# Loads of the later projections issued one or two pairs ahead, and attention of batch 1 entered before batch 0's ends

## The chip, the cores and the metric

The kernel runs on one core of a Trainium2 chip. The metric is the device time of one execution in microseconds (us), as the median of several runs; lower is better. Profiles come from one execution that the hardware profiler recorded.

## The reference

The input x has the shape (batch 4, time 512, 128, 64) in float32. Each (128, 64) slice is a row of D = 8192 features, so x is also (4, 512, 8192). Layer 0 is a sequence model:

```python
xn = layernorm(x.reshape(b, t, d), ln_attn_g, ln_attn_b)
k = xn @ Wk; v = xn @ Wv; r = sigmoid(xn @ Wr)       # 8192 -> 64
s = decay * s + k_t * v_t                            # scan over time -> states
x = x + r * states @ Wo                              # 64 -> 8192
x = x + gelu(conv(layernorm(x), freq_W) + freq_b)    # 3 taps along the 128, 64 -> 64 channels
x = x + layernorm(causal_conv(layernorm(x), time_W) + time_b)   # 3 taps along time, depthwise
x = x + gelu(x @ ffn_W1 + ffn_b1) @ ffn_W2 + ffn_b2  # 64 -> 256 -> 64
```

Layer 1 takes a 25-wide moving average over time off x, transforms the rest with a DFT to 128 modes, multiplies them by complex matrices (one for each of 64 channels), transforms back and adds the average. The change doesn't touch it.

## The kernel before

Layer 0 works on one batch at a time in feature-major tiles: 128 features on the partitions, 512 time steps along them, 64 such chunks in a batch, taken two at a time, so that a batch has 32 pairs. Its stages are Python generators that yield from time to time with a weight for the TensorE work just written:

- J, `project` (L321): the k, v and r projections. Each pair loads its weights (`wkvr`, L342 or L346; from batch 2 on one load for two pairs, 512 KB, into the tag wx with two buffers), the feature-major input (`load_x`, L293, tag xp with three buffers), and a token-major tile of the same input (L349) from which `bn_stats` (L353, two of them, one for each block of 128 tokens) takes the layer norm's statistics. Four scalings of the weights by the norm's gain (L369) and eight matmuls into one PSUM accumulator (L372, each pair's written as four) follow. In batches 2 and 3 the token-major tile lies in the buffers x2 (even pairs) and sq (odd pairs) of the pool `bk`, two buffers each, so that pair k uses the buffer of pair k-4.
- Z, `scan` (L383): `bn_aggr` (L391) makes mean and variance of the statistics, POOL the inverse root (`rsqrt`, L231 and L232), `rows` spreads them over the partitions with TensorE (`spread`, L240) and copies them out with ScalarE (L284), VectorE corrects k, v and r and runs the scan; the moments of the next norm follow from small matmuls (L467, L468).
- A, `attend_and_convolve` (L478): first `rows` for the norm's scale and shift, then for each pair i `attend(i)` (L494 on TensorE, the residual sum L496 and z L500 on VectorE), `convolve(i-2)` (L515, L524, L529; GELU on ScalarE L530, residual L532, squares L535) and `add_up` of pair i-3 (L250), which sums values and squares over the features on TensorE into the accumulator `st`. There is one accumulator bank ("s") for it. When the last sum is out, `begin` is set to b + 1 (L555) and `finish` (L258 to L267) and `moments` give the next norm: the sums are copied out, L262 picks them, L267 copies them as `me`, then come var, `rs` on POOL and mrs.
- C, `convolve_time`, O, `open_feed`, and F, `feed_forward` (L669): the causal convolution with its norm, and the feed-forward part: L678 widens, L682 is the GELU, L689 narrows into the one PSUM buffer "p", L694 evicts it as `x4t` (VectorE), L703 transposes it, and ScalarE copies it out (L710, L712). `convolve_ahead` (L589) does the first fourteen pairs of the next batch's causal convolution inside F; its norm is spread with L240 into "p" too.

`in_turn` (L748) interleaves two lanes of such stages over the list at L788: attention of batch b + 1 runs beside the causal convolution of batch b, projection and scan of batch b + 2 beside the feed-forward part of batch b. A lane steps when its share of work done is behind the other's. Attention of batch 1 may begin only once `begin` is 1, so after the last `add_up` of batch 0.

TensorE executes in the order in which the program is written (`manual_schedule`). On the other engines a scheduler chooses the order, except for instructions given to `keep_in_program_order`: in batches 2 and 3 that is the first `bn_stats` of each pair, not the second. Loads go out on SP's queue in the order that the scheduler gives them, stores on POOL's. An engine executes its instructions in order, so that all that stands behind a waiting one waits too. A load waits for its buffer's last reader.

Of the kernel before, what the change touches and what calls it, by code (L numbers as in the profile page):

```python
# [10 lines left out]
F32 = mybir.dt.float32  # L11
# [5 lines left out]
P = 128  # L17
# [5 lines left out]
SL = 512  # L23
NS = D // SL
NPR = NCH // 2
NT = T // P
S = 64
# [52 lines left out]
def layer0(ctx, tc, dram, x, xt, vecs, wkvr, wo, wdec, wconv, fbias, w1, fb1, w2, fb2, x4):  # L80
# [4 lines left out]
    nc = tc.nc  # L85
# [17 lines left out]
    def two(pool, tag):  # L103
        return pool.tile([P, 2, SL], F32, tag=tag, name=tag)
# [210 lines left out]
    begin = {}  # L315
# [5 lines left out]
    def project(b):  # L321
        pa = two(ps_m, "m") if b == 1 else two(ps_a, "a")
        held[0] = b == 1
        if b == 0:
            psum_w = ps_p.tile([P, SL], F32, tag="p", name="psum_w")
        stt = rowp.tile([P, NT, NS, 6], F32, tag="stt", name="stt")
        for i in range(NPR):
            first, last = i == 0, i == NPR - 1
            if unscanned[0]:

                wq, xk = two(fr, "x1")[:, :, 0 : 4 * S + 3], spare("z", SL)
            elif b == 1:

                both = spare("wx", 4 * S + SL)
                wq, xk = both[:, :, 0 : 4 * S], both[:, :, 4 * S :]
            else:

                xk = two(bk, "sq" if i % 2 else "x2")
                if i % 2 == 0:
                    pairs = spare("wx", 4 * S + SL).rearrange("p k n -> p (k n)")[:, 0 : 16 * S]  # L340
                    pairs = pairs.rearrange("p (c s) -> p c s", c=4)
                    nc.sync.dma_start(pairs, wkvr[2 * i : 2 * i + 4, :, 0 : 4 * S].rearrange("c p s -> p c s"))  # L342
                wq = pairs[:, i % 2 * 2 : i % 2 * 2 + 2, :]
            if b < 2:
                n = 4 * S + 2 * (b == 0)
                nc.sync.dma_start(wq[:, :, 0 : n], wkvr[2 * i : 2 * i + 2, :, 0 : n].rearrange("c p s -> p c s"))  # L346
            xp = load_x(b, i)
            s, h = i // 2, i % 2 * 2
            nc.sync.dma_start(  # L349
                xk, x[b, h * P : (h + 2) * P, s * SL : (s + 1) * SL].rearrange("(t p) d -> p t d", p=P)  # L350
            )
            for t in range(2):
                stats = nc.vector.bn_stats(stt[:, h + t, s, :], xk[:, t, :])  # L353
                if b > 1 and t == 0:

                    tc.keep_in_program_order(stats)
            if b == 0:
                nc.gpsimd.memset(wq[:, :, n:], 1.0)
                for j in range(2):
                    c = 2 * i + j  # L360

                    w = wq[:, j, :]
                    nc.tensor.matmul(
                        psum_w[0 : S + 2, 0 : 4 * S + 3], lhsT=w[:, 3 * S : 4 * S + 2], rhs=w,
                        start=c == 0, stop=c == NCH - 1,
                    )
            for j in range(2):
                w = wq[:, j, 0 : 3 * S]
                nc.vector.tensor_scalar_mul(w, w, vec[:, G1, 2 * i + j : 2 * i + j + 1])  # L369
            for j in range(2):  # L370
                for k in range(2):
                    nc.tensor.matmul(  # L372
                        pa[:, k, :], lhsT=wq[:, j, k * P : (k + 1) * P], rhs=xp[:, j, :],
                        start=first and j == 0, stop=last and j == 1,
                    )
                yield 1.0
        kvrg = rowp.tile([P, 2, SL], F32, tag="kvrg", name="kvrg")
        nc.scalar.copy(kvrg, pa)
        held[0] = False
        projected[b] = (kvrg, stt, psum_w) if b == 0 else (kvrg, stt)  # L380
# [96 lines left out]

    def attend_and_convolve(b):  # L478
        rst, rs, mrs = scanned.pop(b)
        rb, mb = yield from rows(of_a, rs, mrs, "rm")  # L480

        nc.vector.tensor_scalar(mb, mb, at_one[:, 1:2], at_one[:, 0:1], ALU.mult, ALU.add)
        st = ps_s.tile([P, SL], F32, tag="s", name="st")
        free_s[0] = False
        x1s, zs, ws, waiting = {}, {}, {}, {}

        def attend(i):
            xp = load_x(b, i)
            wo_sb = fr.tile([P, P], F32, tag="wo", name="wo_sb")
            nc.sync.dma_start(wo_sb, wo[:, i, :])  # L490
            at = two(ps_a, "a")
            for j in range(2):
                js = slice(j * S, (j + 1) * S)
                nc.tensor.matmul(at[:, j, :], lhsT=wo_sb[js, :], rhs=rst[js, :], start=True, stop=True)  # L494
            x1 = x1s[i] = fr.tile([P, 2, SL], F32, tag="x1", name="x1")
            nc.vector.tensor_tensor(x1, at, xp, ALU.add)  # L496
            z = fr.tile([P, 2, SL], F32, tag="z", name="z", bufs=4)
            for j in range(2):
                zs[2 * i + j] = z[:, j, :]
            nc.vector.tensor_tensor(z, x1, pair_of(rb), ALU.mult)  # L500

        def scaled(i):

            wcs = fr.tile([P, 2, P + H], F32, tag="wcs", name="wcs")
            for j in range(2):
                c = 2 * i + j
                ws[c] = wcs[:, j, :]
                nc.scalar.mul(wcs[:, j, :], wc_sb[:, i % 2, :], vec[:, G2, c : c + 1])

        def convolve(i):  # L510
            cv = c_bank() if i % 2 or held[0] else two(ps_m, "m")
            for h in range(2):
                for j in range(2):
                    q = 32 * (2 * h + j)
                    nc.tensor.matmul(  # L515
                        cv[h * H : (h + 1) * H, j, :], lhsT=cgr[q : q + 2, i, :], rhs=mb[q : q + 2, :],
                        start=True, stop=False,
                    )
            for j in range(2):
                c = 2 * i + j  # L520
                for n, h in neighbours(i % 2, c):
                    if 0 <= n < NCH:
                        rs = halves[rows_of(n // 2 % 2, n - c)]
                        nc.tensor.matmul(  # L524
                            cv[halves[h], j, :], lhsT=ws[n][rs, P:], rhs=zs[n][rs, :], start=False, stop=False
                        )
            for j in range(2):
                c = 2 * i + j
                nc.tensor.matmul(cv[:, j, :], lhsT=ws[c][:, 0:P], rhs=zs[c], start=False, stop=True)  # L529
            nc.scalar.activation(cv, cv, AF.Gelu_apprx_tanh)  # L530
            x2 = two(bk, "x2")
            nc.vector.tensor_tensor(x2, cv, x1s.pop(i), ALU.add)  # L532
            nc.gpsimd.dma_start(x2d[b][2 * i : 2 * i + 2].rearrange("c p t -> p c t"), x2)
            sq2 = bk.tile([P, 2, SL], F32, tag="sq", name="sq2")
            nc.scalar.activation(sq2, x2, AF.Square)  # L535
            for c in (2 * i - 2, 2 * i - 1):
                zs.pop(c, None)
                ws.pop(c, None)
            if i + 2 < NPR:
                scaled(i + 2)  # L540
            waiting[i] = x2, sq2

        for i in range(2):
            scaled(i)
        for i in range(NPR + 3):
            if i < NPR:
                attend(i)
                yield 1.0
            if 1 < i < NPR + 2:
                convolve(i - 2)  # L550
                yield 5.0
            if i > 2:
                add_up(st, i - 3, *waiting.pop(i - 3), i == 3, i == NPR + 2)
                yield 1.0
        begin[attend_and_convolve], free_s[0] = b + 1, True  # L555
        mean3, sq3 = yield from finish(st, of_a, 3)
        carried[b] = moments(mean3, sq3, 3)
# [181 lines left out]


    CHAIN = 6.0

    def run(b, stages):
        for stage, share in stages:
            for weight in stage(b):
                yield weight * share / whole[stage]

    def in_turn(leads, *pairs):  # L748
        at, running = [0.0, 0.0], [None, None]

        def step(k):
            n = int(at[k])
            b, *stages = pairs[n][k]
            if running[k] is None:
                first = stages[0][0]
                if first in needed and b not in needed[first] or begin.get(first, b) < b:
                    return False
                running[k] = run(b, stages)
            share = next(running[k], None)
            if share is None:  # L760
                running[k] = None
                at[k] = n + 1.0
            else:
                at[k] = min(at[k] + share, n + 0.999)
            return True
# [331 lines left out]
```

## Time and profile before

| what | value |
|---|---|
| median of 3 runs | 3829.72 us (3828.04 to 3830.18) |
| the profiled execution: its time | 3831.03 us |
| its span, first to last instruction | 3829.3 us |
| mean granted TensorE clock | 0.981 |
| waits of TensorE on x4t at L689, whole run | 55.3 us in 55 |
| waits of VectorE at `bn_stats` (L353) for the sq loads | 88.2 us in 26 |
| waits of VectorE at `bn_stats` (L353) for the x loads | 56.1 us in 24 |
| waits of VectorE at the scaling (L369) for wx | 81.2 us in 35 |

Engines in the profile: PE is TensorE (PEld its weight loads), DVE VectorE, ACT ScalarE, POOL GpSimd, SP SyncE, whose queue (SPq) issues loads. A number such as L353 is a line of the kernel before. A group such as `stt<-sq` names output and input by the program's names; the token-major tiles of a projection in batches 2 and 3 appear as x and sq. The table of waits lists for an engine, a line and a releaser the total in us, the count and the longest. In a timeline, a line has the start in us from the span's start, the length, the engine and the instruction, and in brackets the idle time ahead of it with what ended it. Busy time is an average over stages with different limits, so stretches of the span are looked at apart. In this execution batch 0's attention ends near 510 us, batch 2's projection runs from about 811 to 1190 us beside batch 0's feed-forward part, and batch 3's begins near 1540 us beside that of batch 1.

### The profile page before, as it was taken

How to read it: one execution, taken by the hardware profiler on the slowest of the kernel's cores; microseconds unless marked ns; L12 is line 12 of the kernel's file. 1: busy time of each engine (PE TensorE's matmuls, PEld its weight loads, DVE VectorE, ACT ScalarE, POOL GpSimd, SP SyncE). 2: the span in 40 equal slices, each digit the busy share in tenths (PEclk: the TensorE clock that was granted, in tenths of full speed). 3: DMA queues.
4: the chain of work that ended last, by engine and by line, in shares of the span. 5: the costliest groups of instructions: out<-in, count | busy, mean ns of one | idle time of the engine just before them, and what ended most of it. 6: DMA issues, size and time to landing. Idle time of an engine off the chain costs nothing. (4 is left out here: it accounts for less than half of the span.)

```text
span 3829.3 us, 44885 instructions
## 1 busy us (share of the span) xinstructions
PE 3620.5 (95%) x15945; PEld 1342.4 (35%) x15945; DVE 2683.1 (70%) x3498; ACT 1763.0 (46%) x2491; POOL 512.9 (13%) x782
## 2 busy tenths in 40 slices
PE   9999998989999999999989988999989999999999
PEld 4433322233333223333322322333322743327533
DVE  4445669975667896677789699845558268892677
ACT  0023346645556565556746578867744210142100
POOL 0000012210001221011121121100013001121001
PEclk9999999999999999999989999999999999999999
DMA  9867647786775687777568677645558368994687
GB/s 311 276 205 242 223 173 250 260 282 229 246 257 182 233 280 271 251 268 278 188 236 290 209 252 256 210 161 179 182 197 285 130 219 292 312 308 148 199 298 263
DMA packets 429175, 912.80 MB, mean 238 GB/s; under 512 B 33240, under 2 KB 83608, under 8 KB 424856
## 3 DMA queue, kind: packets, MB, share of 16 engines
q1 hardware_dynamic: 350656, 636.65, 49.4%
q0 software_dynamic: 75776, 271.62, 20.4%
q8 instruction: 127, 2.08, 0.2%
q10 hardware_dynamic: 2520, 1.67, 0.1%
q14 instruction: 96, 0.79, 0.1%
HBM read 641.31 MB, written 268.50 MB: 238 GB/s over the span
## 5 line engine op out<-in xcount | busy, mean ns | idle before, releaser
L689 PE MATMUL pa<-mid,w_sb 128*64 128x512 f32 x2048 | 499.7, 609 | 55.5 <-DVE x4t L694 55.3
L682 ACT ACTIVATE mid<-m,fb_sb 128x1024 f32<-128x1024 f32 x256 | 285.1, 1114 | 265.2 <-PE m L678 265.0
L694 DVE SCALAR_TENSOR_TENSOR x4t<-pa,fb_sb,x 128x512 f32<-128x512 f32 x252 | 187.7, 745 | 225.6 <-PE pa L689 225.6
L678 PE MATMUL m<-x,w_sb 64*128 64x512 f32 x1008 | 289.4, 647 | 0.8 <-ACT mid L682 0.4
L682 ACT ACTIVATE mid<-c,fb_sb 128x1024 f32<-128x1024 f32 x256 | 283.2, 1106 | 1.0 <-PE c L678 0.9
L678 PE MATMUL c<-x,w_sb 64*128 64x512 f32 x1008 | 263.7, 596 | 9.8 <-ACT mid L682 9.8
L689 PEld LDWEIGHTS pa<-mid,w_sb 128*64 128x64 f32 x2048 | 124.9, 136 | 398.9 <-issue 216.5
L372 PE MATMUL a<-xp,wx 128*128 128x512 f32 x512 | 244.9, 605 | 0.5 <-DVE me L267 0.5
L965 PE MATMUL b<-xin,avg_sb 128*128 128x512 f32 x512 | 230.8, 593 | 3.3 <-DVE xin L971 3.3
L942 ACT COPY two<-a 128x512 f32<-128x512 f32 x64 | 37.5, 586 | 424.7 <-PE a L937 424.7
L971 DVE TENSOR_TENSOR xin<-b,pm 128x512 f32<-128x512 f32 x256 | 159.1, 684 | 95.7 <-PE b L968 80.8
L535 ACT ACTIVATE sq<-x 128x1024 f32<-128x1024 f32 x128 | 135.0, 1055 | 185.6 <-DVE x L532 184.2
L580 DVE SCALAR_TENSOR_TENSOR to<-kd,vec,to 128x510 f32<-128x510 f32 (+1 forms) x272 | 198.2, 748 | 15.1 <-ACT to L576 11.0
L655 ACT ACTIVATE kd<-kd,vec 128x512 f32<-128x512 f32 x256 | 193.3, 809 | 3.1 <-DVE kd L647 3.1
L847 DVE COPY xf<-b 128x256 f32<-128x256 f32 x128 | 54.4, 425 | 189.1 <-PE b L911 188.5
L250 PE MATMUL st<-x,ones 128*32 128x512 f32 x512 | 171.0, 613 | 14.7 <-DVE x L532 14.7
L703 PEld LDWEIGHTS pt<-ident,x4t 128*128 128x128 f32 x1024 | 108.0, 141 | 208.7 <-ACT mid L682 142.8
L494 PE MATMUL a<-rst,wo_sb 64*128 64x512 f32 x512 | 151.8, 667 | 29.5 <-DVE x L496 26.8
L580 DVE SCALAR_TENSOR_TENSOR z<-x,vec,z 128x511 f32<-128x511 f32 x240 | 175.9, 746 | 5.3 <-ACT z L576 2.3
L868 DVE TENSOR_TENSOR uv<-xin 128x1024 f32<-128x1024 f32 x128 | 155.3, 1228 | 33.9 <-DMA edge<-x 13.9
L496 DVE TENSOR_TENSOR x<-a,xp 128x1024 f32<-128x1024 f32 x128 | 156.4, 1222 | 29.3 <-PE a L494 26.5
L703 PE MATMUL pt<-ident,x4t 128*128 128x128 f32 x1024 | 169.0, 288 | 1.5 <-ACT ob L710 1.5
(241 smaller groups left out, 6506.6 us busy)
## 6 DMA issues: line engine op xcount, KB each, us to landing
xp<-in_xt SPq DMA_DIRECT2D x256, 512.0 KB
xin<-x SPq DMA_DIRECT2D x128, 1024.0 KB
kh<-to SPq DMA_DIRECT2D x156, 512.0 KB
x<-x POOLq DMA_DIRECT2D x128, 512.0 KB, 4.5
kx<-x SPq DMA_DIRECT2D x128, 512.0 KB
x<-ob POOLq DMA_DIRECT2D x64, 1024.0 KB, 6.1
out<-xin POOLq DMA_DIRECT2D x64, 1024.0 KB, 6.9
x<-x SPq DMA_DIRECT2D x96, 512.0 KB
```

Of the source, the lines that this page charges most:

```text
L250: nc.tensor.matmul(st[32 * q : 32 * q + 32, :], lhsT=ones, rhs=src[:, j, :], start=first, stop=last,)
L372: nc.tensor.matmul(pa[:, k, :], lhsT=wq[:, j, k * P : (k + 1) * P], rhs=xp[:, j, :], start=first and j == 0, stop=last and j == 1,)
L496: nc.vector.tensor_tensor(x1, at, xp, ALU.add)
L580: tap = nc.vector.scalar_tensor_tensor(to[:, j, k:], xr[:, j, : SL - k], vec[:, w, c], to[:, j, k:], ALU.mult, ALU.add)
L655: tc.keep_in_program_order(nc.scalar.activation(d[:, j, :], d[:, j, :], AF.Identity, bias=vec[:, B4, c], scale=vec[:, G4, c]))
L678: nc.tensor.matmul(pm[:, h, :], lhsT=w1_sb[hs, m * P : (m + 1) * P], rhs=x3[hs, :], start=True, stop=True)
L682: nc.scalar.activation(mid, pm, AF.Gelu_apprx_tanh, bias=fb1_sb[:, m : m + 1])
L689: nc.tensor.matmul(pa[h * H : (h + 1) * H, :], lhsT=w2_sb[:, m, :], rhs=mid[:, h, :], start=(m == 0), stop=(m == 1),)
L694: nc.vector.scalar_tensor_tensor(x4t, pa, fb2_sb, x3s[c // 2][:, c % 2, :], ALU.add, ALU.add)
L703: nc.tensor.transpose(pt[:, t, :], x4t[:, t * P : (t + 1) * P], ident)
L965: nc.tensor.matmul(po[j], lhsT=avg_sb[:, j, :], rhs=xin[:, j, :], start=True, stop=False)
L971: nc.vector.tensor_tensor(by_n(xin[:, j, :]), by_n(po[j]), by_c(pm[j % 2][:, j // 2, :]), ALU.add)
```

## The change

It has two parts.

In `project`, batches 2 and 3 issue their loads in another order. The token-major load of pair i still goes out in step i, but its two `bn_stats` are written two pairs later, in step i + 2 (the last steps' together at the end). The weights of pairs i + 2 and i + 3 are loaded in step i, and `load_x` of pair i + 1 in step i, so that both are ahead of their use by two pairs and one. Buffers and their numbers are as before, and so is the mark that keeps the first `bn_stats` of a pair in program order. Batches 0 and 1 are as they were.

In `attend_and_convolve`, batch 1 may begin before batch 0's attention is done. `begin` gets values between b and b + 1: 0.25 when batch 0's step 32 is done and 0.75 after step 33, 1 at the end. A stage that may not go on yet yields BLOCKED, and `in_turn` then steps the other lane. Batch 1's `rows` are no longer held back by `begin`, its steps 0, 1, 2 and 3 need `begin` at 0.25, 0.5, 0.75 and 1. Its `rows` use another tag, `rm4`, since batch 0 still reads `rm`; and the accumulator `st` is allocated at step 3, when the bank is free again.

```diff
--- before.py
+++ after.py
@@ -324,36 +324,60 @@
         if b == 0:
             psum_w = ps_p.tile([P, SL], F32, tag="p", name="psum_w")
         stt = rowp.tile([P, NT, NS, 6], F32, tag="stt", name="stt")
-        for i in range(NPR):
-            first, last = i == 0, i == NPR - 1
-            if unscanned[0]:
-
-                wq, xk = two(fr, "x1")[:, :, 0 : 4 * S + 3], spare("z", SL)
-            elif b == 1:
-
-                both = spare("wx", 4 * S + SL)
-                wq, xk = both[:, :, 0 : 4 * S], both[:, :, 4 * S :]
-            else:
-
-                xk = two(bk, "sq" if i % 2 else "x2")
-                if i % 2 == 0:
-                    pairs = spare("wx", 4 * S + SL).rearrange("p k n -> p (k n)")[:, 0 : 16 * S]
-                    pairs = pairs.rearrange("p (c s) -> p c s", c=4)
-                    nc.sync.dma_start(pairs, wkvr[2 * i : 2 * i + 4, :, 0 : 4 * S].rearrange("c p s -> p c s"))
-                wq = pairs[:, i % 2 * 2 : i % 2 * 2 + 2, :]
-            if b < 2:
-                n = 4 * S + 2 * (b == 0)
-                nc.sync.dma_start(wq[:, :, 0 : n], wkvr[2 * i : 2 * i + 2, :, 0 : n].rearrange("c p s -> p c s"))
-            xp = load_x(b, i)
+        def token_major(i, xk):
             s, h = i // 2, i % 2 * 2
             nc.sync.dma_start(
                 xk, x[b, h * P : (h + 2) * P, s * SL : (s + 1) * SL].rearrange("(t p) d -> p t d", p=P)
             )
+            return xk
+        def statistics(i, xk):
+            s, h = i // 2, i % 2 * 2
             for t in range(2):
                 stats = nc.vector.bn_stats(stt[:, h + t, s, :], xk[:, t, :])
                 if b > 1 and t == 0:
 
                     tc.keep_in_program_order(stats)
+        def weights(i):
+            if i < NPR:
+                w = spare("wx", 4 * S + SL).rearrange("p k n -> p (k n)")[:, 0 : 16 * S]
+                w = w.rearrange("p (c s) -> p c s", c=4)
+                nc.sync.dma_start(w, wkvr[2 * i : 2 * i + 4, :, 0 : 4 * S].rearrange("c p s -> p c s"))
+                for k in range(2):
+                    ws[i + k] = w[:, 2 * k : 2 * k + 2, :]
+        ws, xps, xks = {}, {}, {}
+        if b > 1:
+            weights(0)
+            xps[0] = load_x(b, 0)
+        for i in range(NPR):
+            first, last = i == 0, i == NPR - 1
+            if b > 1:
+                xks[i] = token_major(i, two(bk, "sq" if i % 2 else "x2"))
+                if i % 2 == 0:
+                    weights(i + 2)
+                if not last:
+                    xps[i + 1] = load_x(b, i + 1)
+                wq, xp = ws.pop(i), xps.pop(i)
+                for k in (i - 2, NPR - 2, NPR - 1) if last else (i - 2,):
+                    if k in xks:
+                        statistics(k, xks.pop(k))
+            else:
+                if unscanned[0]:
+                    wq, xk = two(fr, "x1")[:, :, 0 : 4 * S + 3], spare("z", SL)
+                else:
+                    both = spare("wx", 4 * S + SL)
+                    wq, xk = both[:, :, 0 : 4 * S], both[:, :, 4 * S :]
+                n = 4 * S + 2 * (b == 0)
+                nc.sync.dma_start(wq[:, :, 0 : n], wkvr[2 * i : 2 * i + 2, :, 0 : n].rearrange("c p s -> p c s"))
+                xp = load_x(b, i)
+                statistics(i, token_major(i, xk))
...
@@ -477,11 +501,9 @@
 
     def attend_and_convolve(b):
         rst, rs, mrs = scanned.pop(b)
-        rb, mb = yield from rows(of_a, rs, mrs, "rm")
+        rb, mb = yield from rows(of_a, rs, mrs, "rm4" if b == 1 else "rm")
 
         nc.vector.tensor_scalar(mb, mb, at_one[:, 1:2], at_one[:, 0:1], ALU.mult, ALU.add)
-        st = ps_s.tile([P, SL], F32, tag="s", name="st")
-        free_s[0] = False
         x1s, zs, ws, waiting = {}, {}, {}, {}
 
         def attend(i):
@@ -540,18 +562,26 @@
                 scaled(i + 2)
             waiting[i] = x2, sq2
 
-        for i in range(2):
-            scaled(i)
         for i in range(NPR + 3):
+            while begin[attend_and_convolve] < b + (min(i, 3) - 3) / 4:
+                yield BLOCKED
+            if i < 2:
+                scaled(i)
             if i < NPR:
                 attend(i)
                 yield 1.0
             if 1 < i < NPR + 2:
                 convolve(i - 2)
                 yield 5.0
+            if i == 3:
+                st = ps_s.tile([P, SL], F32, tag="s", name="st")
+                free_s[0] = False
             if i > 2:
                 add_up(st, i - 3, *waiting.pop(i - 3), i == 3, i == NPR + 2)
                 yield 1.0
+            if b == 0 and i >= NPR and i < NPR + 2:
+                begin[attend_and_convolve] = b + (0.25 if i == NPR else 0.75)
         begin[attend_and_convolve], free_s[0] = b + 1, True
         mean3, sq3 = yield from finish(st, of_a, 3)
         carried[b] = moments(mean3, sq3, 3)
@@ -739,11 +769,12 @@
 
 
     CHAIN = 6.0
+    BLOCKED = -1.0
 
     def run(b, stages):
         for stage, share in stages:
             for weight in stage(b):
-                yield weight * share / whole[stage]
+                yield BLOCKED if weight == BLOCKED else weight * share / whole[stage]
 
     def in_turn(leads, *pairs):
         at, running = [0.0, 0.0], [None, None]
@@ -753,10 +784,12 @@
             b, *stages = pairs[n][k]
             if running[k] is None:
                 first = stages[0][0]
-                if first in needed and b not in needed[first] or begin.get(first, b) < b:
+                if first in needed and b not in needed[first]:
                     return False
                 running[k] = run(b, stages)
             share = next(running[k], None)
+            if share == BLOCKED:
+                return False
             if share is None:
                 running[k] = None
                 at[k] = n + 1.0
```

## Prediction

> **What bounds the kernel now.** I read, in this order, the page's busy table, the clock, the table of waits of the whole run, and then the stages one by one, because a share over the whole span hides which stage has idle time to give back.
>
> ```profile
> PE 3620.5 (95%) x15945; PEld 1342.4 (35%) x15945; DVE 2683.1 (70%) x3498; ACT 1763.0 (46%) x2491; POOL 512.9 (13%) x782
> ```
>
> TensorE is busy for 3620.5 of 3829.3 us; only 209 us can be won by removing waits. A second reserve is the clock, granted at 0.981 on average: about 73 us (0.019 of the span). In the table of stretches the columns are: stretch, its length, busy time of PE, PE's loads, DVE, ACT, POOL, granted clock, DMA share, GB/s.
>
> ```profile
> 507.30:519.30 12.00, 7.04 (x37) 2.82 (x32) 5.02 (x5) 4.00 (x7) 0.73 (x1) 1.00 0.22 72
> 519.30:529.50 10.20, 9.75 (x24) 2.49 (x26) 4.07 (x4) 0.10 (x1) 0.00 (x0) 0.50 0.40 142
> ...
> 817.80:826.40 8.60, 3.62 (x12) 2.55 (x12) 3.09 (x11) 0.59 (x1) 1.26 (x2) 0.61 0.74 251
> 900.00:1150.00 250.00, 229.26 (x891) 82.46 (x890) 166.53 (x222) 135.99 (x183) 23.69 (x28) 1.00 0.74 252
> ...
> 1650.00:1900.00 250.00, 249.79 (x1009) 93.06 (x1008) 183.16 (x243) 158.41 (x213) 28.52 (x34) 1.00 0.73 256
> ```
>
> Four places concern this change: the passage from attention of batch 0 to that of batch 1 (507 to 530), the start of batch 2's projection (818 to 826), the body of that stage (900 to 1150, PE idle for 20.7 us), and batch 3's projection (1650 to 1900), where PE is idle for 0.2 us, so nothing that the change does inside it can gain. The waits in 900 to 1150 name the cause of the third (engine, line, releaser; total, times, longest):
>
> ```profile
> DVE stt L353 <- DMA sq<-in_x: 54.8, 9, 7.4
> ...
> DVE stt L353 <- DMA x<-in_x: 26.3, 9, 3.6
> ...
> PE pa L689 <- DVE x4t L694: 15.1, 17, 2.0
> ```
>
> VectorE stands at `bn_stats` for the token-major load, x4t (L694) is queued behind it, and TensorE waits for x4t, since L689 has a single PSUM buffer. The timeline shows one such stall; times are start, length, and the wait before it in brackets:
>
> ```profile
> 1001.75 0.68 DVE L353 BATCH_NORM_STATS2 stt<-sq 128x6 f32<-128x512 f32 x1
> 1009.87 0.69 DVE L353 BATCH_NORM_STATS2 stt<-sq 128x6 f32<-128x512 f32 x1 [7.43 <-DMA sq<-in_x]
> 1010.48 0.73 DVE L694 SCALAR_TENSOR_TENSOR x4t<-pa,fb_sb,x 128x512 f32<-128x512 f32 x1
> ```
>
> The load into sq is issued at 1002.47, as the `bn_stats` that frees its buffer ends, and VectorE's next instruction already needs that load.
>
> **What the Trainium skill says.** "TensorE: Matmul & The Clock Gate", Part 1: The HAM clock gate, says that an array left idle drops to half rate, decided in windows of about 3.4 us. The trace agrees on the window: its half-clock stretches last 3.4, 6.8 or 10.2 us. The page's section on HAM oscillation asks for gaps under about 3.4 us; here the trace is stricter, as two gaps of 1.33 us at 517 and 520 preceded 10.2 us at half clock. "DMA: Bandwidth & Descriptors", Anatomy of one DMA, gives about 2.0 us plus bytes over 436 GB/s (fitted on the software path): an estimate of 3.2 us for 512 KB. The x loads agree (waits up to 3.6 us); sq, queued behind others, takes up to 7.4.
>
> **Part by part.** The sum is made against the profiled execution, 3831.03 us (span 3829.3 and 1.7 around it), which lies 1.3 us above the median. Instruction counts on every engine are unchanged, so only waits and clock are priced. I read the changed order from the built program.
>
> *A. Batch 1's attention inside batch 0's last pairs.* TensorE passed from one batch to the next like this:
>
> ```profile
> 509.09 1.04 PE L250 MATMUL st<-x,ones 128*32 128x512 f32 x2 [1.36 <-DVE x L532]
> ...
> 511.17 1.16 PE L240 MATMUL a<-ident,rs 128*128 128x128 f32 x8
> 513.00 1.16 PE L240 MATMUL a<-ident,mrs 128*128 128x128 f32 x8 [0.68 <-ACT rm L284]
> 514.84 1.13 PE L494 MATMUL a<-rst,wo_sb 64*128 64x512 f32 x4 [0.68 <-ACT rm L284]
> 517.29 1.13 PE L494 MATMUL a<-rst,wo_sb 64*128 64x512 f32 x4 [1.33 <-DVE x L496]
> 519.75 2.08 PE L494 MATMUL a<-rst,wo_sb 64*128 64x512 f32 x4 [1.33 <-DVE x L496]
> 521.76 1.98 PE L515 MATMUL m<-rm,cgr 2*64 2x512 f32 x8
> ```
>
> Idle: 1.36 + 0.68 + 0.68 + 1.33 + 1.33 = 5.38 us. In the new order both spreads (L240) stand before attends of batch 0's last pairs. The first must wait for POOL's rs: I put it at 1.2 us, as TensorE reaches it at about 485.8 and rs is due near 487. Each copy of rm still costs the next attend 0.68, since the bank is the same. Batch 1's first attend now fills the gap ahead of the last sums, of whose 1.36 about 0.45 is left; its second attend waits no longer, its third still does. 1.2 + 0.68 + 0.68 + 0.45 + 1.33 = 4.34: gain 1.0. The gaps are now spread over 30 us with dense work between, so I expect 3.4 us at half clock in place of 10.2: half of 6.8 is 3.4. Part A: -4.4, with bounds 0 (the clock drops as before) and -6.4 (none left at half clock: 1.0 + 5.1, and 0.3 for the estimate of rs). Nothing on other queues moves but two ACT copies.
>
> *B. Start of batch 2's projection.* The opened program issues five statistics loads where it issued seven ahead of the second weights, so these are the eighth load in the queue, not the ninth. This matters because of what stands behind them on DVE:
>
> ```profile
> 820.33 0.32 DVE L369 TENSOR_SCALAR wx<-wx,vec 128x192 f32<-128x192 f32 x1 [2.28 <-DMA wx<-in_wkvr]
> 820.57 0.16 DVE L267 COPY me<-p 128x8 f32<-128x8 f32 x1
> ...
> 822.82 2.08 PE L240 MATMUL p<-ident,rs 128*128 128x128 f32 x8 [4.98 <-POOL rs L232]
> ```
>
> `me` is behind the scaling of wx; me, var, rs and the spread follow. Nine loads from 801.2 to 820.3 are 2.1 us each; one less brings `me` forward by at most that: I take 1.8, as TensorE's L262 ends soon before. The half clock that follows (6.8 us) stays. Later, a stall of 3.1 us at 846 has no counterpart and one of 2.2 at 866 shrinks, of which I credit TensorE 1.0. Part B: -2.8, bounds 0 (another load takes the place) and -7.0 (the whole 4.98, and 2).
>
> *C. The body of batch 2's projection.* Statistics two pairs behind should give each load 25 us. But in the new order, as in the old, the second, unpinned `bn_stats` of pair k-4 stands directly ahead of the first, pinned one of pair k. The load of pair k needs the buffer which that one frees, so VectorE again meets the load just issued. On SP the steady order is the same but for one xp that goes ahead of a kx. The 20.7 us therefore stay: 0. Two more stalls (one sq, one x) come at the end, where the old order had its loads done. In the body a pair of them costs TensorE 20.7 over some ten periods of 25 us, about 2.1; I take +2.4, bounds 0 and +3. The statistics that end two pairs later are read by `bn_aggr` with 9 us to spare (rs at 1190.8, its spread at 1199.69): hidden. In batch 3 the same stalls are under a busy TensorE (0.2 us in 250): 0; without that cover they would cost the same 2.4.
>
> *D. Start of batch 3's projection.* The timelines of VectorE and TensorE have VectorE late here:
>
> ```profile
> 1557.92 0.69 DVE L353 BATCH_NORM_STATS2 stt<-sq 128x6 f32<-128x512 f32 x1 [4.04 <-DMA sq<-in_x]
> 1558.54 0.73 DVE L694 SCALAR_TENSOR_TENSOR x4t<-pa,fb_sb,x 128x512 f32<-128x512 f32 x1
> ...
> 1559.32 1.16 PE L240 MATMUL p<-ident,rs 128*128 128x128 f32 x8 [2.81 <-DVE x4t L694]
> ```
>
> With the first statistics two pairs later, VectorE is spared its waits of 2.00, 0.44 and 4.04 here. TensorE's gaps of 0.68 and 2.81 go (-3.5), and the 3.4 us at half clock that follow at 1560 (-1.7). Part D: -5.2, bounds 0 (the stalls come back one period later and collide with the same spread) and -10 (also the later gaps, 2.37 and 0.92, and the half clock at 1625).
>
> Sum: -4.4 - 2.8 + 2.4 - 5.2 = -10.0, so 3831.0 becomes 3821.0; from the median, 3819.7. The bounds sum to -23.4 and +3.0: 3806.3 to 3832.7.
>
> **Rivals.** (1) Only the places move: the clock drops as before in A, the stalls of B and D recur one period later, C's two are paid. Then -1.0 + 2.4 and nothing else: 3829.7 + 1.4 = 3831. For it: VectorE's total wait does not shrink. Against: the gaps in D rest on a burst of loads which is gone. (2) The change does in C what its words say: the loads land early, 20.7 us in 250 scales to about 25 over the stage, and with the sum above the time is about 3792. For it: order on VectorE is chosen by the scheduler and stalls of x are short. Against: the order puts freeing and using instruction side by side. (3) Slower: xp is now issued right behind sq and wx, and shares the queues with sq. A period on VectorE is 16.7 us of work and 81.1 / 9 = 9.0 of stall, 25.7 us against TensorE's 25; so VectorE is the bound already and each further us of sq's wait is paid. If one 512 KB transfer, 2.1 us, is added in each of 11 periods: +23, less 10 from elsewhere, 3843; it decides as soon as sq's mean wait exceeds 6.1 us (54.8 / 9) by about 1.6 us, where it eats the forecast's gain and reaches +0.2%. Against: xp comes behind sq in the queue, and the DMA share is 0.74.
>
> **Chances.** Forecast 0.56, rival 1 0.28, rival 2 0.04, rival 3 0.12. A measurement can tell about 0.2%, 7.7 us, from no change: faster is below 3822.1, slower above 3837.4. Of the forecast 0.02 falls within. Faster 0.54 + 0.04 = 0.58; same 0.28 + 0.02 = 0.30; slower 0.12. The range 3806 to 3833 is that of the bounds; it holds the forecast and rival 1 and leaves out 0.16.
>
> **What would show it.** Right: in batch 2's stage VectorE still waits about 80 us in 250 at `bn_stats`, sq over x two to one; gaps of about 4 us around A and at most 3.4 us at half clock there; the wait of 4.98 near 3; no wait of 2.81 at batch 3's start. Wrong: `bn_stats` waits that vanish (rival 2), sq waits with a mean of 8 (rival 3), or half-clock time over the whole run that is not shorter by 8 us or more.

## The result: no change, and the profile after

| | before | after |
|---|---|---|
| median of 12 runs | 3828.54 us | 3828.30 us |
| lowest to highest | 3818.39 to 3840.51 | 3819.37 to 3833.78 |
| profiled execution's span | 3829.3 us | 3826.0 us |
| granted clock | 0.981 | 0.981 |

The ratio is 0.9998, with a 95% interval of 0.9988 to 1.0008; a second comparison (below) gave 1.0002, 0.9990 to 1.0014. The forecast was 3819.7, a gain of 10; its range of 3806 to 3833 holds the result, and its first rival ("only the places move", 3831) is nearest to what came. "Same" had been given a chance of 0.30, "faster" 0.58.

In the changed kernel's numbering L494 is L516, L353 is L337, L369 is L393, L689 is L719 and L694 is L724. The busy table first:

```profile
PE 3622.6 (95%) x15945; PEld 1339.1 (35%) x15945; DVE 2681.4 (70%) x3498; ACT 1762.5 (46%) x2491; POOL 510.4 (13%) x782
```

The work is the same. Now the stretches of after that answer to those of before (stretch, length, busy PE, PEld, DVE, ACT, POOL, clock, DMA share, GB/s): the passage between the batches, the start of batch 2's projection, its body, and batch 3's.

```profile
483.40:515.20 31.80, 29.05 (x165) 9.90 (x164) 12.28 (x16) 14.00 (x22) 4.34 (x6) 1.00 0.31 106
515.20:526.00 10.80, 9.43 (x42) 2.42 (x46) 7.29 (x7) 2.57 (x3) 0.72 (x1) 1.00 0.67 208
809.50:818.00 8.50, 5.87 (x26) 4.00 (x26) 5.04 (x12) 0.58 (x1) 1.26 (x2) 0.80 0.62 201
900.00:1150.00 250.00, 228.57 (x888) 82.00 (x887) 167.36 (x224) 136.60 (x183) 23.98 (x28) 1.00 0.74 249
...
1650.00:1900.00 250.00, 249.52 (x1006) 92.56 (x1004) 188.29 (x249) 158.54 (x213) 28.52 (x34) 1.00 0.73 253
```

The body of batch 2's stage has TensorE idle for 21.4 us of 250, as before (20.7). The waits in it, by releaser:

```profile
DVE stt L337 <- DMA sq<-in_x: 53.3, 9, 6.8
...
DVE stt L337 <- DMA x<-in_x: 30.7, 10, 3.1
...
PE pa L719 <- DVE x4t L724: 15.1, 17, 1.6
```

54.8 and 26.3 have become 53.3 and 30.7, and TensorE's 15.1 is 15.1. The timeline of VectorE shows the same pair of instructions as before (start, length; the wait before in brackets), and SP's queue the load between them:

```profile
1015.42 0.68 DVE L337 BATCH_NORM_STATS2 stt<-sq 128x6 f32<-128x512 f32 x1
1022.06 0.69 DVE L337 BATCH_NORM_STATS2 stt<-sq 128x6 f32<-128x512 f32 x1 [5.96 <-DMA sq<-in_x]
1022.67 0.73 DVE L724 SCALAR_TENSOR_TENSOR x4t<-pa,fb_sb,x 128x512 f32<-128x512 f32 x1
```

```profile
1016.13 0.37 SPq L329 DMA_DIRECT2D sq<-in_x  x1
```

The load still goes out as the freeing `bn_stats` ends (1016.1), and the next instruction of VectorE still needs it. That the statistics are written two pairs later has only moved both. The two halves of a tile are read far apart: counted through the loads into sq of this stage, the tile freed at 1016.1 went out at 961.6 and had its first `bn_stats` at 967.0, and its second, which the scheduler may place, stands 48 us behind the first.

The passage between the batches, on TensorE:

```profile
488.15 1.16 PE L240 MATMUL a<-ident,rs 128*128 128x128 f32 x8 [1.10 <-POOL rs L232]
489.98 1.13 PE L516 MATMUL a<-rst,wo_sb 64*128 64x512 f32 x4 [0.68 <-ACT rm L284]
...
497.82 1.13 PE L516 MATMUL a<-rst,wo_sb 64*128 64x512 f32 x4 [0.68 <-ACT rm L284]
...
515.14 1.05 PE L250 MATMUL st<-x,ones 128*32 128x512 f32 x2 [0.30 <-DVE x L554]
...
519.67 1.13 PE L516 MATMUL a<-rst,wo_sb 64*128 64x512 f32 x4 [1.33 <-DVE x L518]
```

1.10 + 0.68 + 0.68 + 0.30 + 1.33 = 4.09 us of idle where there were 5.38. The start of batch 2's projection and that of batch 3's:

```profile
809.89 0.55 DVE L393 TENSOR_SCALAR wx<-wx,vec 128x192 f32<-128x192 f32 x2 [3.59 <-DMA wx<-in_wkvr]
810.35 0.16 DVE L267 COPY me<-p 128x8 f32<-128x8 f32 x1
```

```profile
812.60 1.16 PE L240 MATMUL p<-ident,rs 128*128 128x128 f32 x8 [2.63 <-POOL rs L232]
...
1560.03 1.94 PE L719 MATMUL pa<-mid,w_sb 128*64 128x512 f32 x8 [1.33 <-DVE x4t L724]
...
1565.70 2.08 PE L240 MATMUL p<-ident,mrs 128*128 128x128 f32 x8 [3.14 <-DVE x4t L724]
```

The first wait has fallen from 4.98 to 2.63. At batch 3's start 2.81 did not go: 3.14 stands there now, ahead of the second spread, with 1.33 before it.

### The profile page after: what moved, and what is told of

Read it like the earlier page. It is cut to its first block, busy times and chain, and to the rows that moved or that the text cites. A ratio compares the mean times of both kernels' runs of the same rounds, so it can differ in the third digit from the quotient of the medians.

```text
span 3826.0 us, 44890 instructions
## 1 busy us (share of the span) xinstructions
PE 3622.6 (95%) x15945; PEld 1339.1 (35%) x15945; DVE 2681.4 (70%) x3498; ACT 1762.5 (46%) x2491; POOL 510.4 (13%) x782
## 5 line engine op out<-in xcount | busy, mean ns | idle before, releaser
L719 PE MATMUL pa<-mid,w_sb 128*64 128x512 f32 x2048 | 502.6, 612 | 58.4 <-DVE x4t L724 58.0
L724 DVE SCALAR_TENSOR_TENSOR x4t<-pa,fb_sb,x 128x512 f32<-128x512 f32 x252 | 187.4, 744 | 219.0 <-PE pa L719 218.8
L719 PEld LDWEIGHTS pa<-mid,w_sb 128*64 128x64 f32 x2048 | 125.5, 137 | 404.9 <-issue 215.7
L516 PE MATMUL a<-rst,wo_sb 64*128 64x512 f32 x512 | 150.3, 661 | 27.8 <-DVE x L518 24.4
```

Source lines behind the costliest of these rows:

```text
L719: nc.tensor.matmul(pa[h * H : (h + 1) * H, :], lhsT=w2_sb[:, m, :], rhs=mid[:, h, :], start=(m == 0), stop=(m == 1),)
L724: nc.vector.scalar_tensor_tensor(x4t, pa, fb2_sb, x3s[c // 2][:, c % 2, :], ALU.add, ALU.add)
```

## The experiments

In the table, "idle" is the sum of the gaps between TensorE's matmuls over the whole span, "half" the total length of the stretches granted half the clock, both taken from each trace's records. The last column is span minus idle minus half of "half": nearly what TensorE's work takes at full clock (23 to 31 us of each "half" lie in the gaps themselves and 6 to 9 us behind TensorE's last matmul, of which 2 behind the span's end).

| kernel (profile) | span | idle | half | rest |
|---|---|---|---|---|
| before | 3829.3 | 200.0 | 151.2 | 3553.7 |
| before, again | 3831.1 | 195.9 | 153.1 | 3558.6 |
| after | 3826.0 | 194.6 | 150.1 | 3556.3 |
| after, again | 3820.5 | 193.3 | 139.8 | 3557.3 |
| attention part alone | 3827.6 | 193.9 | 152.3 | 3557.5 |
| the same, again | 3835.3 | 191.7 | 184.2 | 3551.5 |
| projection part alone | 3835.0 | 194.1 | 170.2 | 3555.7 |
| the same, again | 3835.7 | 203.0 | 154.8 | 3555.3 |
| after, both `bn_stats` in order | 3792.0 | 166.7 | 146.7 | 3551.9 |
| the same, again | 3808.0 | 169.3 | 183.9 | 3546.7 |
| before, both in order | 3800.9 | 167.1 | 163.4 | 3552.0 |
| the same with the attention part | 3791.5 | 164.7 | 152.9 | 3550.4 |
| after, both in order in batch 2 only | 3793.0 | 167.1 | 143.9 | 3553.9 |
| before, none in order | 3822.1 | 186.1 | 170.8 | 3550.6 |

The rest is within 12 us for all fourteen, so idle and clock tell a time to about that, not a difference of a few us. The idle time of a kernel repeats within 1 to 9 us; its half-clock time differs by up to 37 us between two profiles of one kernel, 18 us of time.

**The two parts apart.** Each takes one function from the changed kernel and leaves the other as it was.

> The kernel before with the attention part of the change alone. Theory (the attention part takes some 1 to 3 us of idle time off TensorE at the passage from batch 0 to batch 1, and the clock windows only change place): the median of the five waits at that passage sums to about 4.1 us in place of 5.4, total idle time of TensorE 1 to 4 us below the 200 of before, time within 0.15% of before. Rival (the attention part shortens the time by 5 us or more through the clock, and the projection part gives that back): the time is 0.15% to 0.3% below before, and half-clock time is 7 us or more below 151.

Measured: 3827.97 us, ratio 0.9991 (0.9978 to 1.0005); idle at the passage 4.1 us, half-clock time 152.3. Total idle, 193.9, is 6.1 below that of before and so outside the 1 to 4 stated, but before itself moves by 4.1 between two profiles. The rival's shorter clock time is not there.

> The kernel before with the projection part of the change alone. Theory (the stalls at the statistics stay, since order on VectorE still sets the freeing instruction next to the using one): waits at bn_stats stay near 88 us for sq and 56 us for x over the whole run, the wait of TensorE for rs at batch 2's start falls from 4.98 to 2.6 us, one more stall of 2 to 3 us at the end of batch 2's projection, the spread at batch 3's start still waits about 3 us for x4t; time within 0.15% of before. Rival (this part loses what the attention part gains): 0.15% to 0.3% above before.

Measured: 3835.30 us, ratio 1.0011 (0.9999 to 1.0022). Waits at `bn_stats` 89.4 us for sq and 56.2 for x; the wait for rs 2.29; TensorE waits 2.15 us at the end of batch 2's projection, and 2.99 and 2.94 for x4t at batch 3's start. As the theory had it, in the time too, but its interval reaches into the rival's range. Both were run again on another chip:

> The attention part of the change alone, again, on another chip. Theory (1.3 us of idle and, on average, about 4 us of clock at the passage between the batches): ratio to before 0.998 to 0.9995. Rival (nothing but chance in the clock): 0.9995 to 1.0005. In its profile, the waits at the passage sum to 4.1 us again.

Measured: 3830.67 us, ratio 0.9993 (0.9977 to 1.0009), the passage again 4.1 us. The median fits the theory, but the interval takes in the rival and no change at all.

> The projection part of the change alone, again, on another chip. Theory A (it costs some 4 us, as the first comparison had it, 1.0011 with an interval to 0.9999): ratio to before 1.0005 to 1.002. Theory B (it costs nothing and the first was chance): 0.999 to 1.0005. In its profile, idle time of TensorE near 194 us as before; if A, half-clock time above 155 us again (170 in the first profile).

Measured: 3837.00 us, ratio 1.0014 (1.0004 to 1.0024): theory A in the time. Its profile shows no more half-clock time than before has (154.8), and 203.0 us of idle; where the 4 to 5 us lie is therefore not settled. The two stages that this part changes were timed in the traces, from the sums picked at 816.9 in before to the qo matmul of batch 2's scan, and from those picked at 1500.0 to that of batch 3's. With it (four profiles) they take 418.9 and 403.8 us on average, without it (four, all with one `bn_stats` in order) 417.7 and 403.2; single profiles differ by up to 6. The 5.6 us that parts B to D were to save are not there. One part at 0.9991 and 0.9993, the other at 1.0011 and 1.0014, give together 1.0002 to 1.0007, which agrees with what the whole change measured.

**Chance in the clock.** Two kernels as they were:

> The kernel before once more, for a second profile. Theory (a time is TensorE's idle time plus half of its half-clock time plus some 3555 us of work, and the clock part is chance): idle within 5 us of 200, half-clock time different from 151 us by 5 us or more, in other places where the gaps before them are alike, and span minus idle minus half of the half-clock time again between 3551 and 3558. Rival (the clock answers to the gaps alone and so is a property of the kernel): half-clock time within 4 us of 151 and at the same places.

Measured: 3832.83 us in one run; idle 195.9, half-clock 153.1, rest 3558.6. Here the rival's numbers came: the total differs by 1.9, and 22 of the 25 stretches of before have one within 7 us of their place. Four stand where before had none (785 is one), and three of before's are gone; at the wait for rs there were 6.8 us in before and here 3.4, with nearly the same wait (4.98 and 4.61). So most stretches belong to the program and some to chance. How far chance goes, other runs show: the pairs in the table with 152.3 and 184.2, and 146.7 and 183.9, were taken on two chips each, but before's 51 single runs on the chip of the two repeats above were granted 0.977 to 0.982 of the clock, and 0.005 of 3830 is 19 us. The chip is not the reason: over before's single runs the mean is 0.9793 to 0.9796 on each of three. The rest was 0.6 above the stated span.

> The changed kernel once more on this chip, against more runs. Theory (6 us less idle than before, of which chance in the clock leaves nothing to see): ratio to before between 0.998 and 1.001, half-clock time between 145 and 172. Rival (the change is a gain of 0.2% or more that the first comparison missed): ratio below 0.998 with an interval that ends below 1.

Measured: 3830.78 us, ratio 1.0002 (0.9990 to 1.0014). Half-clock time 139.8, 5 below the stated range. The ratio is the theory's.

**What makes the stall.** If the order on VectorE makes it, keeping the second `bn_stats` in program order too must end it, since it then runs two pairs before the load that needs its buffer:

```diff
             for t in range(2):
                 stats = nc.vector.bn_stats(stt[:, h + t, s, :], xk[:, t, :])
-                if b > 1 and t == 0:
+                if b > 1:
                     tc.keep_in_program_order(stats)
```

> The changed kernel with both bn_stats of a pair kept in program order, not only the first. Theory (the stall is a matter of order on VectorE: the freeing statistics of pair k-4 stand directly ahead of the using ones of pair k): waits at bn_stats fall below 30 us for sq and x together over the whole run (144 before), TensorE's waits for x4t in batch 2's stage fall from 16 us to below 6, and the time falls by 12 to 25 us, to 3803 to 3816. Rival (the DMA queues can't bring the loads sooner, so the wait passes to the scaled weights, xp or kh): the time stays within 5 us of before, with waits of VectorE for wx or kh grown by 50 us or more.

Measured: 3792.53 us, ratio 0.9902 (0.9885 to 0.9919), below the expected range. The same stretch of batch 2's stage, then VectorE's timeline and SP's:

```profile
900.00:1150.00 250.00, 249.51 (x982) 91.83 (x982) 186.07 (x244) 151.19 (x205) 27.27 (x32) 1.00 0.79 273
```

```profile
1004.57 0.75 DVE L724 SCALAR_TENSOR_TENSOR x4t<-pa,fb_sb,x 128x512 f32<-128x512 f32 x1 [0.49 <-PE pa L719]
1005.24 1.28 DVE L337 BATCH_NORM_STATS2 stt<-sq 128x6 f32<-128x512 f32 x2
1010.66 0.75 DVE L724 SCALAR_TENSOR_TENSOR x4t<-pa,fb_sb,x 128x512 f32<-128x512 f32 x1 [4.15 <-PE pa L719]
```

```profile
957.57 0.37 SPq L329 DMA_DIRECT2D sq<-in_x  x1
...
982.05 0.37 SPq L329 DMA_DIRECT2D sq<-in_x  x1
...
1006.54 0.37 SPq L329 DMA_DIRECT2D sq<-in_x  x1
```

TensorE is busy for 249.5 of 250 us; VectorE now waits for TensorE (4.15), not TensorE for VectorE. Counted through the stage's loads into sq, the one used at 1005 went out at 957.6, 48 us ahead; the one at 1006.5 goes out as these two end and free its buffer. Waits at `bn_stats` are 2.1 us for sq in the whole run, from 88.7, and 1.0 for x, from 55.4. TensorE's waits for x4t at L719 from 800 to 1190 are 1.5 us; those of before, at L689, are 16.4. Of the rival's sign a part is there: VectorE's waits for the weights at their scaling grew from 81 to 119 us over the run, by 38 and not by 50 or more; 12.8 of them lie between 895 and 1150, where TensorE is idle for 0.5 us all the same. The queues had the bandwidth: 273 GB/s in place of 249.

> The kernel before with both bn_stats kept in program order and nothing of the change. Theory (order alone is the cause; the two pairs of delay are not needed, since the buffer of pair k is then freed four pairs ahead): as for the changed kernel with both kept in order, 8 to 25 us below before, with waits at bn_stats below 60 us together. Rival (the loads need the delay as well): waits at bn_stats stay above 100 us and the time within 5 us of before, while the changed kernel with the same edit is faster by 12 us or more.

Measured: 3800.59 us, ratio 0.9923 (0.9906 to 0.9940); 30 us below before, more than the 8 to 25 stated; one wait of 1.0 us at `bn_stats` for sq and none for x. The edit alone, without the two pairs of delay, does it.

> The kernel before with both bn_stats kept in program order and the attention part of the change, without the projection part. Theory (the 8 us between the two kernels with both kept in order, 3800.6 and 3792.5, come with the attention part, through the clock at the passage between the batches): 3790 to 3796. Rival (they come with the loads given out ahead): 3798 to 3803. No difference at all (chance, or different chips): between these.

Measured: 3793.77 us, ratio 0.9912 (0.9897 to 0.9927). The median fits the theory, but the interval overlaps those of both kernels that it was to tell apart; how much the attention part adds is not shown.

> The changed kernel with both bn_stats kept in program order in batch 2 only, the first alone in batch 3. Theory (in batch 3's projection the same stalls lie under a busy TensorE, as the prediction had it, except at its start): 1 to 5 us above the 3792.5 of the kernel with both kept in order in both batches, TensorE idle below 1 us in 200 us of batch 3's steady part. Rival (the stalls of batch 3 are paid as well): 10 us or more above it.

Measured: 3798.63 us, ratio 0.9917 (0.9902 to 0.9933). The median is 6.1 above 3792.5, outside the 1 to 5 stated, but on another chip; the intervals of the two ratios overlap. From the sums picked at the end of batch 1's attention to the qo matmul of batch 3's scan it takes 403.7 us; with both in order in batch 3 too, 402.6 and 399.9 in two profiles. So batch 3's stalls cost 1 to 4 us here, and this is a difference of two things. From 40 to 140 us behind those sums TensorE is idle for 8.0 us, with both in order for 5.3 and 5.2. At the stage's end, though, the kernels with both in order wait 2.4 us for rs; their last statistics come 361 to 362 us behind the sums, those of the kernels without the projection part 358, where that wait is missing. There the same step takes 402.6 to 403.6 us with one in order (four profiles) and 396.7 and 397.0 with both: 6 us for batch 3's stalls. The steady part hides them: 0.9 us of idle in its last 200 us.

> The changed kernel with both bn_stats kept in program order, again, on another chip: 0.9885 to 0.992 of before, idle time of TensorE near 167 us. If the gain were of that one chip, the ratio would be above 0.995.

Measured: 3798.74 us, ratio 0.9917 (0.9889 to 0.9945), idle 169.3: the gain is not of one chip.

> The kernel before with neither bn_stats kept in program order. The scheduler then draws almost all statistics of a batch to the start of its projection, one load after the other. Theory (a statistics instruction that stands ahead of its load's arrival holds up everything behind it on VectorE): a long stall at the start of batch 2's and batch 3's stages, 50 us or more of waits at bn_stats ahead of the first evictions, and a time 40 to 200 us above before. Rival (VectorE has room there, as it has 30% idle): within 15 us of before.

Measured: 3823.81 us, ratio 0.9978 (0.9966 to 0.9990): faster than before by 0.2%, within the rival's 15 us, and the theory's cost is not there. Statistics waited 30 us in all, 15.9 for sq and 14.3 for x, most of it within the first 100 us of a stage. The spreads at batch 2's start wait 6.15 and 2.38 us for x4t, but the body gains more:

```profile
900.00:1150.00 250.00, 246.87 (x972) 90.44 (x970) 163.59 (x215) 150.73 (x204) 26.76 (x32) 1.00 0.67 233
```

Batch 2's stage is 15.3 us shorter than before, batch 3's, whose stalls were hidden but for its start, 4.2 us longer. Keeping one of the two in order was worse than keeping none.

## Why the prediction was off by its gain

**Part A** (idle -1.0, clock -3.4). The idle term was right: -1.3, with each wait where it was put (1.10 for 1.2, 0.30 for 0.45). The clock term is not borne out. The step "I expect 3.4 us at half clock in place of 10.2" took one profile's stretch for a property of the passage. From the qo matmul of batch 1's scan to the sums picked for batch 0 (474 to 540 in before) the six profiles without the attention part have 6.8 to 23.9 us at half clock, mean 14.2; the eight with it 0 to 23.9, mean 12.4. That is 0.9 us of time less in place of 3.4, and lost in the scatter, which does not exclude the 3.4 either. The part alone measured 0.9991 and 0.9993, some 3 us less, each time with an interval that takes in both -4.4 and 0.

**Part B** (-2.8). The wait for rs fell by 2.35, for which 1.8 was forecast. The three waits for x4t between 845 and 890 sum to 5.58 before and 4.85 after: -0.7 for -1.0. Right in mechanism and size, as far as idle time goes.

**Part C** (+2.4). Right: TensorE's waits for x4t from 895 to 1200 rose from 16.0 to 17.8 us, and the new stall is the last one, a wait for sq of 6.34 on VectorE at 1159.7 that has TensorE wait 2.70 at 1162.3. That the body stays as it was, against what the change says, was the main point and holds; the runs with both in order show the reason. One reading was off: the loads into sq go out every 27.7 us in before (ten of them from 861.9 to 1139.2), so 250 us hold nine periods, not ten of 25 us. Rival 3's period is then 18.5 us of work and 9.0 of stall, 27.5 in all: VectorE works or stalls nearly all of the time. And the statistics that come two pairs later were hidden here, but not once the stalls were gone (the 2.4 us for rs above).

**Part D** (-5.2). Failed. The step "With the first statistics two pairs later, VectorE is spared its waits" counted the stalls of the old order as gone and put none of the new order in their place, though part C had the new order stall in every period. In the trace a wait of 3.27 for x, in front of the eviction at 1564.9, is what the second spread waits for:

```profile
1564.30 0.69 DVE L337 BATCH_NORM_STATS2 stt<-x 128x6 f32<-128x512 f32 x1 [3.27 <-DMA x<-in_x]
1564.91 0.73 DVE L724 SCALAR_TENSOR_TENSOR x4t<-pa,fb_sb,x 128x512 f32<-128x512 f32 x1
```

Between 1540 and 1580 TensorE's waits sum to 4.22 before and 5.26 after, and the half clock there is 6.8 us (from 1565.0) where the forecast had none and before 3.4. The bound of 0 was written for just this.

By place that is -1.3 - 3.1 + 1.8 + 1.0 = -1.6 us of idle for the -4.9 foreseen, and of the clock's -5.1 nothing that can be seen. The median moved by 0.2. Measured alone, the projection part (B, C and D, forecast -5.6) costs 4 to 5 us, in the second run with an interval above 1; so the forecast of -10 failed there first, in D by its mechanism and for the rest by a cause that stays open. That the range holds the result is no credit to the forecast: its upper end is the sum of the bounds for the case that nothing is gained.

**Rivals.** The first came nearest, not in full: D's stall came back and C's last one was paid, but B's did not return, and whether the clock in A drops as before is open. Its price for D should have been the likelier one, as part C's argument was also an argument against D. The third did not come: sq's mean wait in the body is 5.9 us (53.3 / 9), not above 6.1. The second did not come by this change. Its price, "about 3792", is where the kernel with both in order stands (3792.5 and 3798.7), but in part by luck: it is 25 us for the stalls and 12.4 for A, B and D, while order alone, in the kernel before, gave 30, and how much of the rest is the change's is not shown. Of the 37 us by which that kernel's first profile is shorter than before's, 36 lie in batch 2's stage, 29.4 as idle and 5.1 as half of 10.2 us at half clock.

**The skill.** "TensorE: Matmul & The Clock Gate", Part 1: HAM oscillation, asks for gaps below about 3.4 us. As in the first trace, stretches at half clock here follow shorter ones (2.63 us, ended at 812.6; 3.4 us at half clock from 814.1), and not every such gap brings one (3.02 us, ended at 873.6, at full clock). The lengths that the prediction gave were not all: 13.7 and 17.1 us occur in before too, four and five times 3.4. "DMA: Bandwidth & Descriptors", Anatomy of one DMA, gave an estimate of 3.2 us for 512 KB; the wait of 5.96 for sq right behind its issue is again longer than that.

## What to carry to other kernels

Here, to write the use of a load later gained nothing while the instruction that frees its buffer was left to a scheduler that set it next to the use: look in the trace for the load's issue, and count from there to its first user. When an order is fixed by hand, fix all readers of a buffer, not the first alone. And before a stretch at half clock is priced, profile the same kernel twice: here its total changed on its own by 10 to 37 us in four of five kernels, and the forecast counted on 10.2 less.

## What was not expected

A kernel's half-clock time varied from 146.7 to 183.9 us between two profiles with the same instructions, on two chips, and 2.6 us difference in idle; half of those 37 us, 18.6, more than covers the 16 us by which the spans differ. Single runs of before scatter over 3815 to 3850 us. And the kernel with no statistics kept in order, which lets VectorE take the statistics of all of batch 2's pairs within some 100 us (the last aggregation starts at 904.6, and from 800 to 900 the transfers run at 321 GB/s), was faster than the one with half an order.
